# Scattering the experts' rows in waited groups, a later fourth expert, and the last additions on one engine

## The chip, the cores and the metric

The kernel runs on one core of a Trainium2 chip. The metric is the time of one execution on the device, in microseconds (us). The kernel before was run three times: 570.32 us is the median, 569.85 and 570.35 are the ends. One further execution was recorded by the hardware profiler, and all rows below are of that one.

## The reference

A decoder layer in float32 over 16 sequences of 64 tokens (1024 rows of 256): self-attention with 16 heads whose weights come as 4-bit codes with scales, cross-attention with 16 heads over a 64-wide context, and a mixture of experts. Each adds its result to x. The change touches the last part alone:

```python
scores = softmax(xt @ Wg.T)                       # 1024 x 16 experts
# best 2 of 4 groups of experts, then the best 4 experts of those
topi = top_k(masked, 4)[1]
weights = take_along_axis(scores, topi, axis=1)
combine = zeros((T, E)).at[arange(T)[:, None], topi].add(weights)
h = silu(einsum('td,eid->eti', xt, W1)) * einsum('td,eid->eti', xt, W3)   # 176 wide
expert_out = einsum('eti,edi->etd', h, W2)
y = einsum('etd,te->td', expert_out, combine)
z = silu(xt @ Ws1.T) * (xt @ Ws3.T) @ Ws2.T       # shared expert, 352 wide
return y + z
```

## The kernel before

Rows of tokens lie in eight tiles of 128 (`x[0]` to `x[7]`; tiles 0 to 3 are half 0, tiles 4 to 7 half 1). Every float32 operand of a matrix product is split into a high and a low part, and three products of parts stand for one; `parts_of` makes the two parts with a cast on ScalarE (ACT, L112) and a subtract on VectorE (DVE, L113). TensorE is PE, GpSimd is POOL, SyncE is SP.

**The mixture of experts** doesn't compute every expert for every token. Of sixteen experts, the last (`w_last`) is computed for all rows ("dense"), and its share is added by `add_last` (L950 to L954; its add is L952). Each other expert, 0 to 14, has 384 slots in a buffer `xd` in the chip's memory.

1. `send(half)` (L837) scatters the normalised rows of a half to the slots: for each of the four choices k, four indirect transfers of 128 rows each, issued by POOL (L842). The targets are in order of expert, so that choice k can only hold rows of experts from k up. The instructions that write `xd` are kept in `sent_rows`, and for each choice in `sent_for[k]`. `side_by_side` declares that these transfers need not wait for one another.
2. `expert_weights(e)` loads an expert's weights on SP's queue (L277) into one of two buffers with the tag "w123", and splits them into parts: a cast on ACT (L278), a subtract on DVE and one on POOL (L283; DVE for the first three experts).
3. `expert_inputs(e)` loads 384 rows back on SP's queue (L1255), after all transfers in `sent_for[k]` for k up to e have landed, and transposes them on PE: two times three transposes (L1265), each three followed by `parts_of` into `xs`. A small copy, `to` (L1270), keeps the rows' return addresses.
4. `expert_hidden(e)`: eighteen matmuls of 128x384 (the "ups", L104), silu on ACT (L1283, L1286), products on DVE (L1284, L1287), parts `hp`.
5. `send_outputs(e)`: for three blocks of 128 rows, five matmuls each, a copy `y` (L1299), and an indirect transfer on POOL (L1304), which scatters the block to `yd`: rows of a choice lie there by token.
6. `load_outputs(k)` loads the outputs of choice k from `yd`: four transfers of 256 KB on SP's queue (L1320) into buffers with the tag "got", of which there are nine, after every transfer to `yd` that was issued so far (`returned`) has landed. It is called after the sends of expert 11 + k.
7. `add_outputs(k)` adds weight times output to x, one instruction on DVE for a tile (L1334); for tiles 2 and 5 ACT scales (L1331) and POOL adds (L1332). At the end each tile of x is stored (L1392), the even ones by SP's queue and the odd ones by ACT's.

**The order of the work.** A planner puts the instructions of each engine in an order ahead of time, by estimated durations and by the dependences; `tc.issue_after(...)` gives it further bounds. The loop over e from 0 to 16 issues, at step e, the inputs and weights of expert e, the hidden part of expert e - 1 and the outputs of expert e - 2. For e of 1 and 2 the hidden part of the expert before is issued first, and the inputs wait in order for the end of its ups (`up_done`). For e above 2 the inputs are issued before the hidden part of the expert before, so that their transposes can lie among its ups. After the loop come the adds of the four choices and the dense expert's second half (tiles 4 to 7), whose hidden parts are `dense_hidden(w_last, 1, 0)` and `(…, 1, 1)`.

A branch for tokens that find no slot is in the program and is not taken with these inputs.

Of the kernel before, what the change touches and what calls it, by code (L numbers as in the profile page):

```python
# [25 lines left out]
F32 = mybir.dt.float32  # L26
# [3 lines left out]
AF = mybir.ActivationFunctionType  # L30
ALU = mybir.AluOpType
AX = mybir.AxisListType

B, S, D = 16, 64, 256
NT = B * S
NI = NT // 128
# [6 lines left out]
E, INTER, NGRP, TOPK, TOPKG = 16, 176, 4, 4, 2  # L43
# [4 lines left out]
W_COLS = W_UP + 2 * D  # L48
# [23 lines left out]
def decoder_layer(ctx: ExitStack, tc: tile.TileContext, a: dict, out: bass.AP):  # L72
    nc = tc.nc
# [17 lines left out]
    def av_tile():  # L91
        return ps_av.tile([128, 512], F32, tag="av", name="av")
# [24 lines left out]
    x = [t[:, i, :] for t in x_pairs for i in range(2)]  # L117
# [122 lines left out]

    yd = dram.tile([(E - 1) * SLOTS + TOPK * NT, D], F32, tag="yd", name="yd")

    def side_by_side(sent, others):

        for other in others:
            tc.declare_no_dep(sent, other, reason="each writes rows of its own")
        others.append(sent)

    def behind(read, writes):
        for w in writes:  # L250
            tc.add_manual_dep(
                read,
                w.name,
                mybir.DependencyInfo(mybir.DependencyClass.Sync, mybir.DependencyReason.DATA),
                reason="it reads rows of each",
            )
# [42 lines left out]
    def expert_output(ps, w, h_p, cols):  # L299


        w2 = [[p[:, W_UP + k * D : W_UP + (k + 1) * D] for p in w] for k in range(2)]
        h = [p[:, cols] for p in h_p]
        return matmuls(
            ps,
            [
                (h[0], w2[0][0]),
                (h[0], w2[0][1]),
                (h[1], w2[0][0]),
                (h[2], w2[1][0]),  # L310
                (h[2], w2[1][1]),
            ],
        )

    with ExitStack() as attn:
# [410 lines left out]
        rows = [None, None]  # L726
        sent_rows, sent_for = [], [[] for _ in range(TOPK)]
# [108 lines left out]

        def send(half, choices=range(TOPK), waits=()):  # L837

            to = targets[half]
            for k in choices:  # L840
                for i in range(4):
                    sent = nc.gpsimd.indirect_dma_start(  # L842
                        out=xd[: TOPK * NT + (E - 1 - k) * SLOTS],
                        out_offset=bass.IndirectOffsetOnAxis(ap=to[:, k, i : i + 1], axis=0),
                        in_=rows[half][i // 2][:, i % 2, :],
                        in_offset=None,
                    ).ins
                    side_by_side(sent, sent_rows)
                    sent_for[k].append(sent)
                    behind(sent, waits)  # L850

# [107 lines left out]
        with (  # L959
# [109 lines left out]
            def dense_weights():  # L1069

                parts = [
                    xw.tile([128, 2, 2, 4 * HQ], F32R, tag=f"w_q{n}", name=f"w_last{n}")
                    .rearrange("p a b c -> p (a b c)")[:, :W_COLS]
                    for n in range(2)
                ]
                up = xb.tile([128, 3, 2, 2, DC], F32, tag="w_s", name="w_last_up")
                down = xb.tile([128, 2, D], F32, tag="w_o0", name="w_last_down")
                for t, cols in (
                    (up.rearrange("p a b c d -> p (a b c d)"), slice(0, W_UP)),
                    (down.rearrange("p a b -> p (a b)"), slice(W_UP, W_COLS)),  # L1080
                ):
                    nc.sync.dma_start(out=t, in_=a["W123"][E - 1][:, cols])
                    parts_of(t, parts[0][:, cols], parts[1][:, cols])
                return parts
# [18 lines left out]
            def dense_gated(g, up, g2, up2):  # L1103
                h_p = [
                    xa.tile([128, 512], F32R, tag=f"roped1{n}", name=f"dense1{n}", bufs=1)
                    for n in range(2)
                ]
                h_p.append(xa.tile([128, 512], F32R, tag="q_r", name="dense2"))
                nc.vector.tensor_tensor(g, up, g, ALU.mult)
                parts_of(g, h_p[0], h_p[1])  # L1110
                nc.vector.tensor_tensor(g2[:64], up2[64:], g2[64:], ALU.mult)
                parts_of(g2[:64], h_p[2][:64], h_p[2][64:])
                return h_p
# [15 lines left out]
            for n in range(len(units) + 2):  # L1129
# [5 lines left out]
                qd, half = units[min(n, len(units) - 1)]  # L1135
# [52 lines left out]
                if n == 8:  # L1188
                    w_last = dense_weights()
                    with after(exps[-1]):  # L1190
                        routed.append(weights_of_choices(0))
                if n == 9:
# [30 lines left out]
                    with after(aimed, placed):  # L1223
# [4 lines left out]
                        h_p = dense_gated(*dense_ups)  # L1228
# [4 lines left out]
    fw = ctx.enter_context(tc.tile_pool(name="fw", bufs=2, reuse_waits="tile"))  # L1233
    fx = ctx.enter_context(tc.tile_pool(name="fx", bufs=2, reuse_waits="tile"))
    fh = ctx.enter_context(tc.tile_pool(name="fh", bufs=2, reuse_waits="tile"))
    fy = ctx.enter_context(tc.tile_pool(name="fy", bufs=2, reuse_waits="tile"))

    gated, up_done = [None], [None]

    def expert_weights(src, down_lo=nc.gpsimd):  # L1240
        return weight_parts(
            src,
            fw.tile([128, W_COLS], F32, tag="w123", name="w123"),
            [
                fw.tile([128, W_COLS], F32R, tag=f"w123{n}", name=f"w123{n}", bufs=3)
                for n in range(2)
            ],
            down_lo,
        )
# [63 lines left out]

    def load_outputs(k):

        tiles = []
        for n in range(NI // 2):
            t = fy.tile([128, 2, D], F32, tag="got", name="got", bufs=9)
            first = (E - 1) * SLOTS + (TOPK - 1 - k) * NT + n * 256
            got = nc.sync.dma_start(  # L1320
                out=t, in_=yd[first : first + 256].rearrange("(i p) d -> p i d", p=128)
            ).ins
            behind(got, returned)
            tiles.append(t)
        return tiles

    def add_outputs(k, got, cw):
        for i in range(NI):
            y, w = got[i // 2][:, i % 2], cw[i // 4][:, k, i % 4 : i % 4 + 1]
            if i % 3 == 2:  # L1330
                nc.scalar.activation(y, y, AF.Copy, scale=w)  # L1331
                nc.gpsimd.tensor_tensor(x[i], x[i], y, ALU.add)  # L1332
            else:
                nc.vector.scalar_tensor_tensor(x[i], y, w, x[i], ALU.mult, ALU.add)  # L1334

    def dense_hidden(w, half, n):
        return expert_hidden(w, [p[:, :, n * 256 : n * 256 + 256] for p in normed[half]], 256)

    def dense_output(w, h_p, half, n, add):
        for b in range(2):  # L1340
            ps = av_tile()[:, :D]
            expert_output(ps, w, h_p, slice(b * 128, b * 128 + 128))
            add(half, 2 * n + b, ps)
# [6 lines left out]
    ws, xs, hs, got = {}, {}, {}, {}  # L1350
    with tc.issue_after(lows[-1]), tc.issue_after(silus[-1]):
        ws[0] = expert_weights(a["W123"][0], nc.vector)
    for e in range(E + 1):
        if e in (1, 2):

            low = lows[-1]
            hs[e - 1] = expert_hidden(ws[e - 1], xs[e - 1][0], SLOTS)
        if e < E - 1:
            low = lows[-1]
            with tc.issue_after(up_done[0] if e in (1, 2) else low):  # L1360
                xs[e] = expert_inputs(e)
            if e >= 1:
                with tc.issue_after(low), tc.issue_after(silus[-1]):
                    ws[e] = expert_weights(a["W123"][e], nc.vector if e < 3 else nc.gpsimd)
        if e == 1:
            with tc.issue_after(gated[0]), tc.issue_after(silus[-1]):
                routed.append(weights_of_choices(1))
        if 0 <= e - 1 < E - 1 and e > 2:
            hs[e - 1] = expert_hidden(ws[e - 1], xs[e - 1][0], SLOTS)
        if e - 2 >= 0:  # L1370
            if e == E:

                with tc.issue_after(gated[0]):
                    h_p = dense_hidden(w_last, 1, 0)
            last = send_outputs(e - 2, ws.pop(e - 2), hs.pop(e - 2), xs.pop(e - 2)[1])
            if e - 2 == E - TOPK - 2:
                short = slots_are_short()
            k = e - 2 - (E - 1 - TOPK)
            if k >= 0:
                got[k] = load_outputs(k)  # L1380
    with ExitStack() as behind_last:
        for ins in (*last, gated[0]):
            behind_last.enter_context(tc.issue_after(ins))
        cw = [r[0] for r in routed]
        add_outputs(0, got[0], cw)
        dense_output(w_last, h_p, 1, 0, add_last)
        add_outputs(1, got[1], cw)
        dense_output(w_last, dense_hidden(w_last, 1, 1), 1, 1, add_last)
        for k in range(2, TOPK):
            add_outputs(k, got[k], cw)  # L1390
    for i in range(NI):
        (nc.sync if i % 2 == 0 else nc.scalar).dma_start(  # L1392
# [10 lines left out]
    with tc.If(short > 0):  # L1403
        w_over = [weights_without_slot(half, routed[half][2]) for half in range(2)]
        with tc.For_i(0, E - 1, 1) as e:
            w = expert_weights(a["W123"][bass.ds(e, 1)].rearrange("o p c -> p (o c)"))
            for half in range(2):
                dense_expert(w, half, add_over)

                t = fs.tile([128, 4, E], F32, tag="slot", name="w_next")  # L1410
# [105 lines left out]
```

## Time and profile before

| What | us |
|---|---|
| median of three runs | 570.32 |
| the profiled execution | 577.4 |
| its span, from the first instruction to the last | 575.5 |
| PE busy in the span | 540.3 (94%) |
| DVE busy | 400.2 (70%) |
| ACT busy | 279.3 (49%) |
| POOL busy | 230.6 (40%) |
| 16 sends of half 1 to `xd`, first start to last start | 439.40 to 460.24 |
| first output send of expert 0, last of expert 14 | 472.70, 556.00 |
| loads of the four choices, issued from | 544.41, 551.41, 554.70, 561.03 |
| the adds of the end on DVE | 552.59 to 571.16 |

Positions are microseconds from the start of the span. The mean granted clock of TensorE was 0.978 of the full one. A row of a timeline gives the start, the duration, the engine, the line of the kernel, the operation, the result and operands by the program's names, and in brackets how long the engine was idle before it and what ended that. A row of groups gives after the bar the busy time, the mean in ns of one instruction, and the idle time before them. A row of stretches gives for 10 us the busy time of each engine. In the rows of slices each digit is a fortieth of the span, in tenths busy.

### The profile page before, as it was taken

What the parts mean: (1) busy time and instruction counts of PE and PEld (TensorE: products, weight loads), DVE (VectorE), ACT (ScalarE), POOL (GpSimd) and SP (SyncE); (2) the same over time, 40 slices, a digit from 0 to 9 for tenths busy, and PEclk for the clock granted to TensorE, in tenths of its full rate; (3) what the DMA queues carried; (4) which work ended last, traced back from release to release, by engine and by line L of the source; (5) the groups of instructions that cost most, each with busy time, mean ns of one, the idle gap of its engine ahead of it and who ended that gap; (6) DMA issues with size and microseconds to landing.
All of it is one profiled execution on the core that took longest, in us unless ns stands there. A gap on an engine that the chain in (4) does not pass through costs nothing.

```text
span 575.5 us, 10603 instructions
## 1 busy us (share of the span) xinstructions
PE 540.3 (94%) x4013; PEld 446.7 (78%) x4013; DVE 400.2 (70%) x879; ACT 279.3 (49%) x524; POOL 230.6 (40%) x213
## 2 busy tenths in 40 slices
PE   7999999999999989999999999999999779999962
PEld 5889898888989876757778577685787669999951
DVE  6355566644655788848577586889777479999866
ACT  4677557575574431230432323152525187777551
POOL 4260500101001005426243444632544717888862
PEclk9999999999999999999999999999999789999995
DMA  8564431823200599482020000000511658777384
GB/s 227 145 166 146 111 109 39 227 86 112 75 1 1 167 250 308 111 239 52 2 70 1 8 1 1 0 31 0 188 50 68 202 169 285 240 245 238 122 279 152
DMA packets 56294, 70.83 MB, mean 123 GB/s; under 512 B 13872, under 2 KB 42768, under 8 KB 56240
## 3 DMA queue, kind: packets, MB, share of 16 engines
q1 hardware_dynamic: 51408, 58.71, 34.5%
q0 software_dynamic: 3696, 10.36, 4.7%
q10 hardware_dynamic: 1136, 1.05, 0.6%
q8 instruction: 33, 0.54, 0.4%
q14 instruction: 21, 0.17, 0.1%
HBM read 48.61 MB, written 21.86 MB: 122 GB/s over the span
## 4 chain that ended last, share of the span: by engine, by line
PE 81%; DVE 7%; issue 4%; DMA 3%; ACT 3%; POOL 1%; SPq 1%; DVEq 0%; ACTq 0%; POOLq 0%
PE mm L104 47%; PE mm L1005 7%; PE av L590 5%; PE av L104 5%; PE at L573 4%; PE at L343 3%; PE at L1028 2%; PE av L1041 2%; PE at L1265 2%; PE mm L439 2%; DMA bqkv<-in_bqkv 1%; PE mm L461 1%; DMA got<-yd 1%; DVE x L1334 1%; POOL roped L990 1%
## 5 line engine op out<-in xcount | busy, mean ns | idle before, releaser
L990 POOL TENSOR_TENSOR roped<-rt,rt 128x512 f32<-128x512 f32 x48 | 62.6, 1325 | 83.4 <-DVE rt L984 80.5
L984 DVE TENSOR_TENSOR rt<-mm,rope_q 128x512 f32<-128x512 f32 x96 | 61.4, 685 | 24.3 <-PE mm L104 23.6
L104 PE MATMUL mm<-xn,w_q 128*128 128x512 f32 x288 | 73.9, 403 | 0.5 <-ACT xn L222 0.5
L104 PEld LDWEIGHTS mm<-xn,w_q 128*128 128x128 f32 x288 | 52.2, 188 | 14.0 <-issue 1.8
L104 PE MATMUL mm<-xs,w 128*128 128x384 f32 x270 | 55.3, 354 | 7.0 <-ACT xs L112 5.8
L1304 POOL DMA_INDIRECT yd<-y,to x45 | 47.9, 1064 | 27.6 <-ACT y L1299 13.1
L104 PEld LDWEIGHTS mm<-xs,w 128*128 128x128 f32 x270 | 48.4, 198 | 9.0 <-ACT xs L112 6.6
L327 ACT ACTIVATE p<-p 128x512 f32<-128x512 f32 x32 | 20.1, 629 | 62.3 <-DVE p L326 62.3
L324 DVE TENSOR_REDUCE sm_m<-at 128x8 f32<-128x512 f32 x32 | 21.8, 680 | 37.1 <-PE at L573 36.2
L1005 PE MATMUL mm<-roped,w_s 128*64 128x512 f32 x192 | 46.4, 602 | 0.7 <-POOL roped L990 0.7
L522 POOL TENSOR_TENSOR wv<-code,scale 128x512 fp32r<-128x512 f32 x7 | 9.5, 1360 | 88.2 <-DMA scale<-in_scales 58.7
L613 DVE TENSOR_TENSOR x<-mm,x 128x256 f32<-128x256 f32 x64 | 26.0, 419 | 23.9 <-PE mm L104 21.9
L104 PE MATMUL mm<-wo,o 128*128 128x256 f32 x256 | 39.6, 295 | 0.0
L104 PE MATMUL av<-w,hp 128*128 128x256 f32 x225 | 35.2, 290 | 0.7 <-ACT y L1299 0.7
L104 PE MATMUL mm<-xn,wq 128*128 128x512 f32 x128 | 34.6, 405 | 0.7 <-ACT xn L222 0.5
L104 PE MATMUL mm<-wv,xn 128*128 128x256 f32 x256 | 35.2, 289 | 0.0
L104 PE MATMUL mm<-xn,wk 128*128 128x512 f32 x128 | 34.9, 404 | 0.0
L590 PE MATMUL av<-pt,v 128*128 128x128 f32 x256 | 34.5, 277 | 0.0
L104 PEld LDWEIGHTS mm<-wo,o 128*128 128x128 f32 x256 | 32.9, 190 | 1.5 <-issue 0.4
L590 PEld LDWEIGHTS av<-pt,v 128*128 128x128 f32 x256 | 32.0, 191 | 1.2
L104 PEld LDWEIGHTS mm<-wv,xn 128*128 128x128 f32 x256 | 31.8, 189 | 0.9
L104 PEld LDWEIGHTS av<-w,hp 128*128 128x128 f32 x225 | 30.6, 190 | 1.9 <-ACT y L1299 1.2
(216 smaller groups left out, 1145.8 us busy)
## 6 DMA issues: line engine op xcount, KB each, us to landing
w<-in_W SPq DMA_DIRECT2D x15, 640.0 KB
code<-in_codes SPq DMA_DIRECT2D x32, 256.0 KB
scale<-in_scales SPq DMA_DIRECT2D x32, 256.0 KB
xr<-xd SPq DMA_DIRECT2D x15, 408.0 KB
xd<-zeros SPq DMA_DIRECT2D x8, 720.0 KB
yd<-zeros SPq DMA_DIRECT2D x8, 512.0 KB
got<-yd SPq DMA_DIRECT2D x16, 256.0 KB
wq<-in_Wq SPq DMA_DIRECT2D x4, 512.0 KB
```

The lines of the kernel that those rows point to most:

```text
L104: m = nc.tensor.matmul(ps, lhsT=l, rhs=r, start=(n == 0), stop=(n == len(pairs) - 1))
L324: nc.vector.tensor_reduce(m, sc, AX.X, ALU.max)
L327: exps.append(nc.scalar.activation(p, p, AF.Exp, scale=scale).ins)
L343: last = nc.tensor.transpose(ps[:, 2 * n : 2 * n + 2, :].rearrange("p a q -> p (a q)"), pn[:, 2 * n : 2 * n + 2, :].rearrange("p a k -> p ...
L439: nc.tensor.matmul(ps[:, c * DCQ : (c + 1) * DCQ], lhsT=wq[:, h, c * 128 : (c + 1) * 128], rhs=wkq[:, h, :], start=True, stop=True,)
L573: nc.tensor.matmul(sc[par * 64 : par * 64 + 64, 2 * g + pp, :], lhsT=qk[0][:, b * S : (b + 1) * S], rhs=qk[1][:, b * S : (b + 1) * S], sta ...
L590: nc.tensor.matmul(av[:, k * 128 : (k + 1) * 128], lhsT=v[:, i, k0 : k0 + HD], rhs=pt[:, i].rearrange("p a q -> p (a q)"), start=True, sto ...
L613: nc.vector.tensor_tensor(x[i], ps, x[i], ALU.add)
L984: nc.vector.tensor_tensor(mt, ps3, rope_table(t, 2 * ab + k), ALU.mult)
L990: nc.gpsimd.tensor_tensor(r.rearrange("p (b s) -> p b s", s=S), one, two, op)
L1005: nc.tensor.matmul(ps[h // 2][(h % 2) * 64 : (h % 2) * 64 + 64], lhsT=w_s[:, t, blk, ab, :], rhs=roped[2 * t + ab], start=first[h], stop=l ...
L1304: sent = nc.gpsimd.indirect_dma_start(out=yd[: (E - 1) * SLOTS + min(TOPK, E - 1 - e) * NT], out_offset=bass.IndirectOffsetOnAxis(ap=to[:, ...
```

## The change

1. In `send`, the first transfer and the others of a group of four wait, for half 1 and choices 1 to 3, for the landing of the last transfer of the group before: `side_by_side` leaves that one out of the declaration.
2. For e of 3 too the hidden part of the expert before is issued first, and the inputs of expert 3 are issued after the end of expert 2's ups.
3. `add_outputs` does all tiles by the one instruction on DVE.
4. The outputs of the last choice (k of 3) are loaded into the two weight buffers "w123", two of 256 KB in each, and the second and fourth load are issued by ACT's queue.
5. The first two tiles of the dense expert's second half are issued before the adds of the first choice, and the other two before those of the second.

```diff
-    def side_by_side(sent, others):
+    def side_by_side(sent, others, landed=()):
         for other in others:
-            tc.declare_no_dep(sent, other, reason="each writes rows of its own")
+            if other not in landed:
+                tc.declare_no_dep(sent, other, reason="each writes rows of its own")
         others.append(sent)
...
             for k in choices:
+                landed = sent_rows[-1:] if half and k else ()
                 for i in range(4):
...
-                    side_by_side(sent, sent_rows)
+                    side_by_side(sent, sent_rows, landed)
...
     def load_outputs(k):
-        tiles = []
-        for n in range(NI // 2):
-            t = fy.tile([128, 2, D], F32, tag="got", name="got", bufs=9)
+        if k == TOPK - 1:
+            tiles = [
+                t[:, n * 2 * D : (n + 1) * 2 * D].rearrange("p (i d) -> p i d", i=2)
+                for t in (fw.tile([128, W_COLS], F32, tag="w123", name="got_last") for _ in range(2))
+                for n in range(2)
+            ]
+        else:
+            tiles = [
+                fy.tile([128, 2, D], F32, tag="got", name="got", bufs=9) for _ in range(NI // 2)
+            ]
+        for n, t in enumerate(tiles):
             first = (E - 1) * SLOTS + (TOPK - 1 - k) * NT + n * 256
-            got = nc.sync.dma_start(
+            got = (nc.scalar if k == TOPK - 1 and n % 2 else nc.sync).dma_start(
                 out=t, in_=yd[first : first + 256].rearrange("(i p) d -> p i d", p=128)
             ).ins
             behind(got, returned)
-            tiles.append(t)
         return tiles
...
-            if i % 3 == 2:
-                nc.scalar.activation(y, y, AF.Copy, scale=w)
-                nc.gpsimd.tensor_tensor(x[i], x[i], y, ALU.add)
-            else:
-                nc.vector.scalar_tensor_tensor(x[i], y, w, x[i], ALU.mult, ALU.add)
+            nc.vector.scalar_tensor_tensor(x[i], y, w, x[i], ALU.mult, ALU.add)
...
     for e in range(E + 1):
-        if e in (1, 2):
+        if e in (1, 2, 3):
             low = lows[-1]
             hs[e - 1] = expert_hidden(ws[e - 1], xs[e - 1][0], SLOTS)
         if e < E - 1:
             low = lows[-1]
-            with tc.issue_after(up_done[0] if e in (1, 2) else low):
+            with tc.issue_after(up_done[0] if e in (1, 2, 3) else low):
                 xs[e] = expert_inputs(e)
...
-        if 0 <= e - 1 < E - 1 and e > 2:
+        if 0 <= e - 1 < E - 1 and e > 3:
             hs[e - 1] = expert_hidden(ws[e - 1], xs[e - 1][0], SLOTS)
...
+        dense_output(w_last, h_p, 1, 0, add_last)
         add_outputs(0, got[0], cw)
-        dense_output(w_last, h_p, 1, 0, add_last)
-        add_outputs(1, got[1], cw)
         dense_output(w_last, dense_hidden(w_last, 1, 1), 1, 1, add_last)
-        for k in range(2, TOPK):
+        for k in range(1, TOPK):
             add_outputs(k, got[k], cw)
```

## The prediction

> **What bounds the kernel now.** I read, in order, the busy shares and the forty slices, the chain that ended last, the table of 10 us stretches from 430 us on (the only part that the change touches), and then the timelines of single engines around 460 to 480 us and from 552 us.
>
> ```profile
> PE 540.3 (94%) x4013; PEld 446.7 (78%) x4013; DVE 400.2 (70%) x879; ACT 279.3 (49%) x524; POOL 230.6 (40%) x213
> ...
> PE   7999999999999989999999999999999779999962
> DVE  6355566644655788848577586889777479999866
> PEclk9999999999999999999999999999999789999995
> ...
> PE 81%; DVE 7%; issue 4%; DMA 3%; ACT 3%; POOL 1%; SPq 1%; DVEq 0%; ACTq 0%; POOLq 0%
> ```
>
> TensorE sets the time, and is below nine tenths in two places after the start: slices 32 and 33 (about 446 to 475 us, where the experts' rows are sent and the first experts start) and the last two. The stretches say the same:
>
> ```profile
> 450.00:460.00 10.00, 7.87 (x34) 7.21 (x34) 5.48 (x13) 1.45 (x3) 7.95 (x7) 0.66 0.62 207
> 460.00:470.00 10.00, 6.68 (x34) 6.45 (x34) 6.98 (x21) 7.49 (x12) 0.96 (x1) 0.83 0.64 220
> 470.00:480.00 10.00, 8.62 (x57) 7.87 (x56) 9.70 (x21) 7.89 (x17) 6.09 (x6) 1.00 0.59 181
> 480.00:490.00 10.00, 10.00 (x74) 10.00 (x73) 9.18 (x17) 8.40 (x18) 6.63 (x7) 1.00 0.83 277
> 500.00:510.00 10.00, 10.00 (x70) 9.84 (x69) 9.69 (x16) 7.54 (x16) 8.74 (x7) 1.00 0.76 256
> 560.00:570.00 10.00, 3.21 (x10) 2.36 (x10) 9.84 (x19) 2.59 (x6) 4.05 (x5) 0.50 0.62 195
> ```
>
> (Busy us of PE, PEld, DVE, ACT, POOL, then granted clock, DMA share, GB/s.) From about 474 to 540 us PE and DVE are full, and POOL is close to it: time lost before it is not made up there, and time saved before it is kept. From 560 us it is DVE that is full.
>
> **A, sends by fours.** Three waits on POOL, no instruction more. Before, the sixteen sends of half 1 start 1.26 to 1.33 us apart, and then POOL has nothing to do:
>
> ```profile
> 460.24 0.96 POOL L842 DMA_INDIRECT xd<-rows,to  x1 [0.30 <-issue]
> 472.70 0.95 POOL L1304 DMA_INDIRECT yd<-y,to  x1 [11.50 <-ACT y L1299]
> ```
>
> By the semaphores' events the last send of each group landed 2.3, 3.4, 3.2 and 3.1 us after its start. So: the second choice's group starts at 445.9 (landing of the first's last) instead of 444.8, its last send starts at 449.7 and lands at 453.0; the third's lands at 460.1; the fourth's last starts at 463.9 and lands at 467.0, POOL is free at 464.9 instead of 461.2 (+3.7). Behind the waiting sends on POOL stands expert 0's first output send, wanted at 472.70: 7.8 us of cover. The loads of expert rows (L1255) on SP wait for the landings: expert 1's row load goes out at about 453.1 instead of 452.4 and lands at 457.3, needed by the transposes at 459.19; expert 2's at 460 to 461.5, needed at 469.02; expert 3's at 467 to 468, landing 471, needed at about 476. On SP the loads of weights stand behind these (w for expert 2 now ahead of expert 1's rows). Cost 0; without the cover up to 3.7. It could also gain: with one group in flight less, a landing may shorten, but nothing waits for it.
>
> **B, expert 3's rows later.** Moved behind expert 2's ups: one load of 408 KB on SP (now behind expert 3's weights), six transposes, two casts on ACT, two subtracts and the copy of `to` on DVE. Nothing is added. Before, three of the transposes ran inside expert 2's ups, and PE went on without a hole:
>
> ```profile
> 463.24 0.79 PE L104 MATMUL mm<-xs,w 128*128 128x384 f32 x3 [3.23 <-ACT xs L112]
> 471.41 0.80 PE L104 MATMUL mm<-xs,w 128*128 128x384 f32 x3 [1.10 <-ACT xs L112]
> 473.56 0.55 PE L1265 MATMUL at<-ident,xr 128*128 128x128 f32 x3
> 473.87 1.81 PE L104 MATMUL mm<-xs,w 128*128 128x384 f32 x9
> 475.64 0.49 PE L1265 MATMUL at<-ident,xr 128*128 128x128 f32 x3
> ```
>
> The first two lines are what this order costs: experts 1 and 2 have it already, with all six transposes after the ups of the one before, and their ups start 3.23 and 1.10 us late, behind an ACT cast. Expert 3 now gets it too. On ACT, before, its work came ahead of expert 2's silu:
>
> ```profile
> 473.25 1.26 ACT L278 CAST w<-w 128x1280 fp32r<-128x1280 f32 x1 [0.16 <-PE av L104]
> 474.42 0.47 ACT L112 CAST xs<-at 128x384 fp32r<-128x384 f32 x1
> ```
>
> After, ACT does the two silus first (0.50 + 0.48, the second ready at about 477.0, when the ups end), then the weights' cast (1.26, to 478.3), then the rows' (0.48 each, to 479.4), with the DVE subtract (0.51) behind. PE has meanwhile the transposes (0.82) and a part of expert 1's fifteen output matmuls (2.1 us if all are left, near nothing if they were already drawn ahead). So the hole is between 0.9 and 2.7 us; I take 1.8, between the two rows. Some 0.2 comes back, as the pieces of DVE and ACT work of the next step are done in it: 1.6 late. Who is late next: expert 3's ups, its outputs and sends, then each expert behind, by PE's order. To take it back, experts 4 to 14 would have to run faster than a pair per 11.7 us, and they have nothing to do so with: POOL has three sends at 1.26 plus a subtract of 1.31 to 2.06 for each, PE 9.6 to 10 of 10. Ends: 0 (the work hides wholly under expert 1's outputs) and 2.7. Which experts have their transposes inside the ups of which others shifts by one up to the end; I cost this at 0, with ±0.6 (half of the 1.10 row) for the last expert's start.
>
> **C, D, E, the end.** Removed: 8 ACT scales (505 ns) and 8 POOL adds. Added: 8 DVE adds. Moved: four loads of the last choice into weight buffers, two from SP's queue to ACT's; the dense outputs of the last expert (four L952 adds, ten matmuls) ahead of the first choice's adds in issue.
>
> ```profile
> L1334 DVE SCALAR_TENSOR_TENSOR x<-got,cw,x 128x256 f32<-128x256 f32 x24 | 12.5, 576 | 2.5 <-DMA got<-yd 2.4
> L1332 POOL TENSOR_TENSOR x<-x,got 128x256 f32<-128x256 f32 x8 | 6.1, 778 | 4.5 <-ACT got L1331 2.7 <-DVE x L952 0.9 <-DVE x L1334 0.8
> ...
> 563.39 1.83 DVE L1334 SCALAR_TENSOR_TENSOR x<-got,cw,x 128x256 f32<-128x256 f32 x2
> 565.25 0.97 DVE L113 TENSOR_TENSOR hp<-h,hp 64x256 fp32r<-64x256 f32 x1
> 569.50 1.66 DVE L1334 SCALAR_TENSOR_TENSOR x<-got,cw,x 128x256 f32<-128x256 f32 x4
> ```
>
> The last line is the undisturbed pace: starts 0.395 us apart. The two above it lie beside POOL adds and take twice as long; summed over the tail the stretched ones lose 3.0 us. The rule that speaks against C is in the Trainium skill, "Perfetto Trace Analysis", "Optimizing Scalar/DVE Operations": where DVE is saturated, giving work to ScalarE or even GpSimd can pay, though GpSimd and DVE share a port, so between these two it may not. DVE is saturated here (9.84 of 10). By the first half of the rule, taking eight adds back costs 8 x 0.395 = 3.2; by the rows, 3.2 - 3.0 = +0.2. I go by the rows.
>
> E only changes the order of issue; PE is idle for 4.23 us there, ahead of its matmuls at 560.86: 0. Where the adds end: the third choice's first load landed at 559.5, held by sends and transfers that don't change, and behind it DVE has 27 instructions after (21 before): 559.6 + 27 x 0.395 = 570.3. The last choice's loads wait for the last expert's sends to land (560.94), not for a buffer, so new buffers don't start them earlier; two queues may bring the last of them from 566.8 to about 565.5 (the third choice's end at 562.3, and 1 MB at the 0.8 us per 256 KB seen there). As their adds come early in DVE's order I allow a stall of 0.6. So the last add ends at 570.9, against 571.16: -0.3. On ACT, the cast of `hp` 64x256 (561.39 before) stands behind two loads that wait for 560.94: 0.6 late, with the last dense outputs behind it, before at 568.32: covered. Ends for the end: -2.0 (all stretching gone, no stall) and +1.5 (a stall of 2.4, as the 2.38 us wait for a load before 558.62 shows).
>
> **Sum.** A 0, B +1.6, end -0.3: +1.3 us on the profiled execution's 577.4 (575.5 between first and last instruction, 1.9 around them; the last add is 4.3 ahead of the span's end, and the output stores behind it stay). That execution is 7.1 us above the median of the runs, 570.32; as I carry only a difference of a part at the full clock, it goes over unscaled: 571.6.
>
> **The rivals.** Bound for "no change": 0.2%, 1.14 us, about what a measurement of this kernel can tell.
> - Late fourth expert kept to the end (above), 571.5 to 573: 0.40.
> - Nothing moves, 570.5: the hole is below 1 us, since DVE's and ACT's work for expert 3 fills it, and the end gives 0.3 back. For it: PE has 7 output matmuls to spare at 472.48. Against it: the rows of 3.23 and 1.10 had such matmuls as well. 0.28.
> - Other side, the end wins, 568.4: DVE with no POOL add beside it keeps 0.395 all through, and the two queues bring the last loads before DVE asks, -2.0, and the hole is near 0. It decides from the point where the end gains over 1.1 more than the hole costs. For it: six stretched lines. Against: 27 instructions behind 559.5. 0.22.
> - DVE becomes the bound of the end, 573.6: hole 2.0, and adds of the last choice placed ahead of others stall DVE, +1.3. 0.10.
>
> **How the numbers follow.** Faster is the third case: 0.22. Same is the second: 0.28. Slower: 0.40 + 0.10 = 0.50. Range 568.6 to 573.9: the cut faster case at the low end, the fourth case at the high, a tenth left out at each. The first case alone: 571.5 to 573.
>
> **What would show it.** A: half 1's sends in four groups with gaps of 1 to 3 us, expert 0's first output send at 472.7 still held by ACT's y. B: a wait of 0.9 to 2.7 us on ACT's xs ahead of expert 3's first three ups at about 477, and the last expert's sends later by as much. End: every DVE add at 0.42 to 0.48, no POOL after the last send, the last add 0.3 us earlier than the sends' lag would make it. Wrong if PE is as full at 470 to 480 as before, or if the last sends come no later, or if DVE waits for the last loads by over 1 us.

## The result, and the profile after

The changed kernel takes 572.85 us (median of five, 571.93 to 574.24) against 569.85 (569.52 to 570.35) before: 0.54% longer, 95% interval 0.42 to 0.66%. Measured again beside parts of the change it was 573.0 against 569.73: 0.66%, 0.45 to 0.88%. So it costs 3.0 to 3.3 us, where 1.3 were forecast; the sign and the range held.

Before takes about 570 us in most measurements, but the profiled execution of the first part took 577.4 and one set of runs below about 577 (the longest executions there, up to 589 us, are left out of the medians), so each kernel is compared with before as measured beside it, and traces with a second trace of before, of 569.12 us.

The page of the changed kernel (profiled execution 574.24 us):

```profile
span 572.5 us, 10586 instructions
...
PE 536.0 (94%) x4013; PEld 443.5 (77%) x4013; DVE 400.1 (70%) x887; ACT 276.1 (48%) x516; POOL 223.1 (39%) x205
...
PE   6999999999999989999999999999999769999961
...
DVE  5455556644565789758486686889778677999876
...
PE 70%; DVE 7%; POOL 7%; DMA 7%; issue 6%; ACT 2%; SPq 0%; DVEq 0%; POOLq 0%; ACTq 0%
PE mm L104 40%; PE mm L1009 7%; PE av L592 5%; POOL xd L846 5%; PE at L575 4%; PE at L345 2%; PE av L104 2%; PE at L1032 2%; PE mm L441 2%; PE av L1045 2%; DMA xd<-rows,to 2%; DMA yd<-y,to 1%; DMA bqkv<-in_bqkv 1%; POOL yd L1308 1%; PE mm L463 1%
```

The sends to `xd` are now on the chain that ended last: POOL at L846 with 5% of the span, and their landings with 2%. The stretches of 10 us (PE, PEld, DVE, ACT, POOL, granted clock, DMA share, GB/s) show PE's dent deeper at 460 us than in the second trace of before, here first:

```profile
450.00:460.00 10.00, 8.00 (x45) 7.05 (x45) 6.71 (x21) 6.10 (x10) 6.62 (x7) 1.00 0.68 223
460.00:470.00 10.00, 7.63 (x50) 6.83 (x50) 8.64 (x18) 8.13 (x16) 4.69 (x4) 1.00 0.90 290
470.00:480.00 10.00, 10.00 (x71) 9.97 (x70) 9.10 (x19) 7.93 (x17) 6.51 (x7) 1.00 0.88 281
```

and then the changed kernel:

```profile
450.00:460.00 10.00, 7.33 (x44) 6.80 (x45) 6.48 (x20) 6.23 (x10) 4.74 (x5) 1.00 0.37 136
460.00:470.00 10.00, 6.12 (x39) 5.17 (x37) 7.44 (x17) 6.59 (x13) 6.77 (x7) 1.00 0.69 230
470.00:480.00 10.00, 9.22 (x57) 9.22 (x58) 6.77 (x13) 6.58 (x15) 6.59 (x6) 0.83 0.93 330
```

PE is busy for 22.67 of these 30 us instead of 25.63. The timelines name it. POOL of the changed kernel, the first send of each waiting group, the last send and the first output send:

```profile
443.78 1.06 POOL L846 DMA_INDIRECT xd<-rows,to  x1 [1.73 <-DMA xd<-rows,to]
452.62 0.96 POOL L846 DMA_INDIRECT xd<-rows,to  x1 [3.48 <-DMA xd<-rows,to]
459.35 0.95 POOL L846 DMA_INDIRECT xd<-rows,to  x1 [1.73 <-DMA xd<-rows,to]
463.14 1.67 POOL L846 DMA_INDIRECT xd<-rows,to  x1 [0.30 <-issue]
465.12 0.96 POOL L1308 DMA_INDIRECT yd<-y,to  x1 [0.31 <-ACT y L1303]
```

and, in the second trace of before, the last send of half 1 and the same first output send:

```profile
457.48 0.96 POOL L842 DMA_INDIRECT xd<-rows,to  x1 [0.30 <-issue]
464.65 0.95 POOL L1304 DMA_INDIRECT yd<-y,to  x1 [6.20 <-ACT y L1299]
```

PE of the changed kernel, the transposes of experts 1, 2 and 3:

```profile
455.17 0.85 PE L1269 MATMUL at<-ident,xr 128*128 128x128 f32 x6 [2.43 <-DMA xr<-xd]
462.69 0.85 PE L1269 MATMUL at<-ident,xr 128*128 128x128 f32 x6 [2.32 <-DMA xr<-xd]
470.78 1.09 PE L1269 MATMUL at<-ident,xr 128*128 128x128 f32 x6 [2.07 <-DMA xr<-xd]
```

In the second trace of before:

```profile
454.31 0.85 PE L1265 MATMUL at<-ident,xr 128*128 128x128 f32 x6 [1.37 <-DMA xr<-xd]
461.88 0.84 PE L1265 MATMUL at<-ident,xr 128*128 128x128 f32 x6 [1.77 <-DMA xr<-xd]
465.69 0.55 PE L1265 MATMUL at<-ident,xr 128*128 128x128 f32 x3 [0.19 <-DVE xs L113]
466.00 1.81 PE L104 MATMUL mm<-xs,w 128*128 128x384 f32 x9
```

PE waits for the rows in both; expert 3's rows come just in time before, and 2.07 us late after, although their transposes now stand later in PE's order. To compare traces whose starts differ, I use three distances in us: from the first send of half 1 to the first output send of expert 0 (E0), from the same first send to the last output send of expert 13, and from that last output send to the end of the last add.

| Kernel | first send to E0 | first send to last send of expert 13 | from there to last add |
|---|---|---|---|
| before, first trace | 33.3 | 111.9 | 19.9 |
| before, second trace | 27.5 | 106.3 | 19.1 |
| eight adds alone, second run | 27.5 | 107.2 | 19.0 |
| end alone | 27.5 | 107.1 | 20.2 |
| expert 3 later alone | 27.5 | 108.8 | 19.0 |
| expert 3 later, and the end | 27.5 | 108.5 | 21.4 |
| waits alone | 28.5 | 114.0 | 18.8 |
| waits alone, queue as before | 27.6 | 112.6 | 20.2 |
| last wait alone | 27.5 | 110.3 | 19.1 |
| waits and expert 3 later | 28.2 | 110.5 | 19.0 |
| changed, first trace | 28.2 | 110.2 | 20.5 |
| changed, second trace | 29.1 | 109.9 | 19.9 |

Each row is one trace. Kernels that are alike in the middle column's part (before's second trace, adds, end) differ there by up to 0.9 us. In the last column the kernels with the end of before lie at 18.8 to 19.1, but two of them at 19.9 and 20.2, and the changed kernel's two traces are 0.6 apart. Differences that are no larger than these say nothing by themselves.

### The profile page after: what moved, and what is told of

The parts are those of the page before. It is cut to its first block, busy times and chain, and to the rows that moved or that the text cites. A ratio compares the mean times of both kernels' runs of the same rounds, so it can differ in the third digit from the quotient of the medians.

```text
span 572.5 us, 10586 instructions
## 1 busy us (share of the span) xinstructions
PE 536.0 (94%) x4013; PEld 443.5 (77%) x4013; DVE 400.1 (70%) x887; ACT 276.1 (48%) x516; POOL 223.1 (39%) x205
## 4 chain that ended last, share of the span: by engine, by line
PE 70%; DVE 7%; POOL 7%; DMA 7%; issue 6%; ACT 2%; SPq 0%; DVEq 0%; POOLq 0%; ACTq 0%
PE mm L104 40%; PE mm L1009 7%; PE av L592 5%; POOL xd L846 5%; PE at L575 4%; PE at L345 2%; PE av L104 2%; PE at L1032 2%; PE mm L441 2%; PE av L1045 2%; DMA xd<-rows,to 2%; DMA yd<-y,to 1%; DMA bqkv<-in_bqkv 1%; POOL yd L1308 1%; PE mm L463 1%
## 5 line engine op out<-in xcount | busy, mean ns | idle before, releaser
L104 PE MATMUL mm<-xs,w 128*128 128x384 f32 x270 | 53.9, 344 | 2.2 <-ACT w L280 1.3
L104 PEld LDWEIGHTS mm<-xs,w 128*128 128x128 f32 x270 | 46.0, 190 | 4.1 <-ACT w L280 2.2
L104 PEld LDWEIGHTS mm<-wv,xn 128*128 128x128 f32 x256 | 31.8, 189 | 0.9
```

The lines of the kernel that those rows point to most:

```text
L104: m = nc.tensor.matmul(ps, lhsT=l, rhs=r, start=(n == 0), stop=(n == len(pairs) - 1))
```

## The experiments

Line numbers of the changed kernel are 2 to 7 higher than those of before.

### Before once more

No edit.

> The kernel before once more, for a second trace. In the first one TensorE's granted clock fell to 0.66 in 450 to 460 us and to 0.83 in 460 to 470, and POOL's first send of half 1 stood 5.3 us behind the targets, where the changed kernel's trace has clock 1.00 and 3.5 us. Theory 'rows' (the sends by fours make TensorE wait for the rows of experts 1 to 3): without the drop in the clock the span is 2 to 4 us shorter than 575.5, and TensorE's waits on the row loads (DMA xr) ahead of the transposes of experts 1 to 3 sum to under 3 us, against the 7.2 of the changed kernel. Theory 'planner' (the later fourth expert costs the time): the waits on xr are 5 us or more here too.

569.12 us, span 567.3: 8.2 us shorter than in the first trace, where 2 to 4 were expected. The waits of TensorE on the row loads between 436 and 482 us (in us: sum, number, longest) are

```profile
PE at L1265 <- DMA xr<-xd: 3.7, 3, 1.8
```

and in the changed kernel's first trace

```profile
PE at L1269 <- DMA xr<-xd: 7.2, 4, 2.4
```

Of these 1.37 + 1.77 = 3.1 us belong to experts 1 to 3: a little over the 3 us expected, while the 'planner' theory wanted 5 or more. The changed kernel's second trace has 4.9 us in all, 1.2 more than before and not 3.5; there the clock fell to 0.75 in 455 to 460 us behind a wait of 2.97, and nine ups took 3.06 us, so that a part of the loss shows as slow matmuls instead of waits. The first trace of before had none of these waits. There PE stood still for another reason before the rows could be missed:

```profile
450.68 1.13 PE L104 MATMUL mm<-ws,sh 96*128 96x256 f32 x4 [1.65 <-issue]
```

and its clock was 0.66 in 450 to 460, so that expert 0 was 5.8 us later against the sends (first column of the table). That trace showed slack where the second has none.

### The waits alone

```diff
+    def side_by_side(sent, others, landed=()):
+        for other in (o for o in others if o not in landed):
...
+                    side_by_side(sent, sent_rows, sent_rows[-1 - i :][:1] if half and k else ())
```

> Only the waits of the sends in half 1, by fours; each engine's order stays, but on SP's queue expert 1's rows stand behind expert 2's weights and expert 3's weights ahead of expert 3's rows. Theory 'rows': slower by 1.5 to 2.5 us, TensorE waits about 2 us on xr at each of experts 1, 2 and 3. Theory 'planner', and the record's own step A: within 0.5 us of before.

576.16 us against 569.79: 1.16% slower (1.01 to 1.32), 6.4 us, over twice what I expected. The place is expert 3's three transposes, which in this order stand in front of fifteen of expert 2's eighteen ups:

```profile
470.93 0.87 PE L1265 MATMUL at<-ident,xr 128*128 128x128 f32 x3 [4.33 <-DMA xr<-xd]
471.45 3.23 PE L104 MATMUL mm<-xs,w 128*128 128x384 f32 x9
```

Behind the wait of 4.33 us the nine ups took 3.23 us; in the second trace of before the same nine took 1.81. The granted clock of the stretch (the value behind POOL's) says why:

```profile
470.00:475.00 5.00, 4.07 (x15) 4.10 (x16) 1.55 (x3) 0.48 (x1) 1.45 (x1) 0.50 1.06 396
```

So the waiting was paid once as idle time and once more as a halved clock. The Trainium skill, "TensorE: Matmul & The Clock Gate", "What's actually happening", has it that an idle window of about 3.4 us sets the array to half speed; this wait was longer, and the clock was at half. In the first trace of the changed kernel the clock fell too (0.83 in 470 to 480) where no single wait was over 2.4 us, so the length of one wait isn't all of it. The run with the last wait alone, below, shows it more plainly: nine ups took 3.23 us behind a wait of only 2.06.

### Expert 3's rows later alone

```diff
-        if e in (1, 2):
+        if e in (1, 2, 3):
...
-            with tc.issue_after(up_done[0] if e in (1, 2) else low):
+            with tc.issue_after(up_done[0] if e in (1, 2, 3) else low):
...
-        if 0 <= e - 1 < E - 1 and e > 2:
+        if 0 <= e - 1 < E - 1 and e > 3:
```

> Only expert 3's rows behind expert 2's ups, and the order that follows from it. The record's step B: +1.6 us, a hole of 0.9 to 2.7 us ahead of expert 3's ups. Theory 'rows': within 0.5 us of before, since TensorE then waits for rows at about this place anyway, or not at all.

571.11 against 569.79: 0.27% slower (0.14 to 0.41), 1.3 us by the medians. The prediction's step B holds: the hole at expert 3's ups was there,

```profile
471.53 0.79 PE L104 MATMUL mm<-xs,w 128*128 128x384 f32 x3 [0.83 <-ACT xs L112]
```

of 0.83 us (0.9 to 2.7 expected), and the last send of expert 13 comes 1.5 to 2.4 us later against the first send, so it is not made up behind.

### The end alone

All of `load_outputs`, `add_outputs` and the order of the end as in the change; nothing else.

> Only the end: all adds on VectorE, the last choice's loads into the weights' buffers over two queues, the dense outputs ahead in order. The record's step: -0.3 us. Theory 'end' (eight more adds behind the third choice's landing aren't given back): +0.7 us, as the changed kernel's last add ends 20.5 us behind the last send of expert 13, and 19.9 before.

570.54 against 569.79: 0.23% slower (0.11 to 0.35), 0.75 us by the medians. Theory 'end' fits in size. DVE of this kernel towards the end:

```profile
548.76 0.48 DVE L1337 SCALAR_TENSOR_TENSOR x<-got,cw,x 128x256 f32<-128x256 f32 x1
549.27 0.42 DVE L1287 TENSOR_TENSOR h<-mm,g 64x256 f32<-64x256 f32 x1
549.73 0.88 DVE L952 SCALAR_TENSOR_TENSOR x<-av,cl,x 128x256 f32<-128x256 f32 x2
552.56 0.88 DVE L1337 SCALAR_TENSOR_TENSOR x<-got,cw,x 128x256 f32<-128x256 f32 x2 [1.96 <-DMA got<-yd]
```

At 552.56 it takes up the third choice's first tile, after 1.96 us of waiting. By the program's order six adds of the first two choices still stand behind it (tiles 4 and 5 of the first, tiles 4 to 7 of the second).

### The waits and expert 3's rows later

Both edits above, the end as before.

> The waits by fours and expert 3's rows later, the end as before. Alone they cost 6.4 and 1.3 us. Theory 'cover' (with expert 3's transposes behind expert 2's ups, TensorE runs these eighteen matmuls while expert 3's rows are on their way, so that the wait of 4.3 us which they had in front of the ups shrinks to about 2): +1.5 to +2.5 us. Theory 'sum' (two independent costs): +7 to +8 us, which the end would have had to give back by 4 to 5.

575.18 against 576.86: 0.36% faster (0.19 to 0.53), where both theories expected it slower. They were meant against 570, and before took 577 here, so the total tests neither of them; the distance does. The last send of expert 13 comes 110.5 us behind the first send: 3.5 us less than with the waits alone (114.0), and 1.7 more than with expert 3 later alone (108.8). That fits theory 'cover' and not 'sum': alone the two cost 7.7 and 2.4 in this distance, together 4.2. The wait for expert 3's rows is 2.44 us here, behind expert 2's ups, not 4.33 in front of fifteen of them.

### The waits, with SP's queue as before

```diff
+        ).ins; loads.append(load)
...
-                with tc.issue_after(low), tc.issue_after(silus[-1]):
+                with tc.issue_after(low), tc.issue_after(silus[-1]), tc.issue_after(loads[e * 2 - 3] if e in (2, 3) else low):
```

> The waits by fours, with SP's queue held in the order of before (expert 1's rows ahead of expert 2's weights), so that the order of every engine is that of before and only the three waits are added. Theory 'weights' (the 640 KB of expert 2's weights, loaded 5 us earlier, lie among the second choice's rows and make them land late, 3.75 us of wait): the third group's wait falls to 2 us or less, everything behind comes 1.5 to 2 earlier, +4 to +5 us. Theory 'waits' (the three landings themselves): +6 to +6.8 as with the queue changed.

576.72 against 576.86, no difference (0.08% faster, from 0.23% faster to 0.07% slower), where 4 us or more were expected; before took 577 here too, so this total tests nothing either. By the traces, the waits of the sends on landings in this kernel:

```profile
POOL xd L842 <- DMA xd<-rows,to: 4.0, 2, 2.2
```

and in the one with the waits alone:

```profile
POOL xd L842 <- DMA xd<-rows,to: 5.5, 2, 3.7
```

The long wait, for the second choice's rows, falls from 3.75 to 2.23 us when expert 2's 640 KB of weights are not loaded among them, nearly to what 'weights' said, and the distance to expert 13's last send falls from 114.0 to 112.6. So, by one trace each, the load in front of the landing costs about 1.5 us of the distance, and the rest, 5.3 to 6.2, is the waits themselves.

### The eight adds alone, twice

```diff
-            if i % 3 == 2:
-                nc.scalar.activation(y, y, AF.Copy, scale=w)
-                nc.gpsimd.tensor_tensor(x[i], x[i], y, ALU.add)
-            else:
-                nc.vector.scalar_tensor_tensor(x[i], y, w, x[i], ALU.mult, ALU.add)
+            nc.vector.scalar_tensor_tensor(x[i], y, w, x[i], ALU.mult, ALU.add)
```

> Only the eight adds moved to VectorE. Theory 'end' (VectorE is the bound behind the third choice's loads): the stretched instructions, 3.1 us in the second trace of before, go; eight times 0.395 come: 0 to +1 us. The record's step gave +0.2.

576.08 against 576.86: 0.08% faster, from 0.29% faster to 0.13% slower. Once more, where before took 569.73:

> Only the eight adds moved to VectorE, once more. All of the end together cost 0.8 to 1.3 us where before ran at 570. Theory 'adds': +0.5 to +1.2, VectorE works without a gap from the third choice's load to the end and no instruction is stretched. Theory 'loads' (what costs is the last choice's loads, by their place in ScalarE's and SP's order): within 0.4 of before.

568.99 against 569.73: 0.08% faster, from 0.20% faster to 0.04% slower. So the adds are not what the end costs. The group of this kernel's adds (busy us, mean ns of one, idle us before them):

```profile
L1330 DVE SCALAR_TENSOR_TENSOR x<-got,cw,x 128x256 f32<-128x256 f32 x32 | 13.4, 478 | 2.0 <-DMA got<-yd 2.0
```

against, in the second trace of before,

```profile
L1334 DVE SCALAR_TENSOR_TENSOR x<-got,cw,x 128x256 f32<-128x256 f32 x24 | 13.2, 605 | 2.1 <-DMA got<-yd 2.0
```

32 adds at 478 ns keep DVE busy hardly longer (13.4 us) than 24 at 605 ns (13.2): what DVE does more, it had lost before in adds that took longer beside POOL's.

### The last choice's loads alone

The edit of `load_outputs` alone.

> Only the last choice's loads in the weights' buffers and over two queues, the adds as before. ScalarE's scales of tiles 2 and 5 and the cast of hp stand behind its two loads, which wait for the last expert's sends. Theory 'blocked ScalarE': +0.5 to +1.5 us. Theory of the record: 0, since the loads' start is set by the sends and their end is early enough.

577.53 against 576.86: 0.16% slower, from 0.04% faster to 0.36% slower. That holds both theories and doesn't decide between them.

### The changed kernel without the waits, and with them

The changed kernel once more:

> The changed kernel beside the parts of it, on one chip. From the first send of half 1 to the last output send of expert 13 its first trace has 110.2 us, before (second trace) 106.3, the waits alone 114.0 to 114.9, expert 3's rows later alone 108.8. Theory 'cover': 110 to 110.6 again, and +2.5 to +3.5 us against before where before runs at about 570. Where before itself runs at about 577 (TensorE's stall of 1.65 us at 449 us and the fallen clock behind it, as in the first trace), the waits keep that stall away, and the changed kernel is level with before or up to 2 us faster.

573.0 against 569.73: 0.66% slower (0.45 to 0.88), 3.3 us; distance 109.9. Without the waits of the sends:

> The changed kernel without the waits of the sends. Theory 'cover' (with expert 3's rows later, the waits cost only what lies beyond the hole that the later rows make anyway): the waits' own share of the change is 1 to 2 us, so this is 1 to 2 us faster than the changed kernel where before runs at about 570, with 108.5 to 109.2 us from the first send to expert 13's last. Theory 'waits are free inside the change' (the record's step A, if expert 3's order covers them): within 0.5 of the changed kernel.

572.25: 0.48% slower than before (0.32 to 0.64), 2.5 us; distance 108.5. The waits' own share inside the change is thus 0.75 us by the medians, 1.4 by the distances: between the two theories, and far from the 6.4 that the waits cost alone. It isn't clear of noise: the two kernels were run six times each, from 571.94 to 575.52 us and from 571.61 to 573.21.

### The last wait alone

```diff
+                    side_by_side(sent, sent_rows, sent_rows[-1 - i :][:1] if half and k == 3 else ())
```

> Only the wait ahead of the fourth choice's four sends; expert 3's weights move ahead of expert 3's rows on SP's queue, every other engine's order is that of before. The fourth group starts about 2.5 us later. In the second trace of before, expert 3's rows were there just in time (the transposes waited 0.2 us, for VectorE). Theory 'just in time' (each us that expert 3's rows land later is one that TensorE stands in front of expert 2's ups): +1.5 to +3 us. Theory 'slack' (the record: rows at 471, needed at 476): within 0.5 of before.

572.68 against 569.73: 0.55% slower (0.39 to 0.71), 3.0 us, at the upper end of 'just in time'. The fourth group started after a wait of 3.85 us, and PE waited for expert 3's rows as with all the waits, only for less:

```profile
468.59 0.87 PE L1265 MATMUL at<-ident,xr 128*128 128x128 f32 x3 [2.06 <-DMA xr<-xd]
469.12 3.23 PE L104 MATMUL mm<-xs,w 128*128 128x384 f32 x9
```

Behind it the same nine ups took 3.23 us again; the clock was 0.65 in 465 to 470 and 0.67 in 470 to 475. There was no slack at expert 3's rows.

## Why the prediction was right, and where it was not

**The sum.** Forecast +1.3, measured +3.0 and +3.3. The number is in the range of the likeliest case (the late fourth expert kept to the end, 571.5 to 573), but in part by luck: the late expert came at 1.3 us, which by itself would have lain just under that range (571.1), and the rest came from two terms that the forecast put at nothing and at a gain.

**A, the waits: 0 forecast, 0.75 us measured inside the change, 6.4 alone.** The step that failed is "expert 1's row load ... lands at 457.3, needed by the transposes at 459.19; expert 2's at 460 to 461.5, needed at 469.02; expert 3's at 467 to 468, landing 471, needed at about 476". Counted from the first send, expert 3's rows were to be loaded at about 28 us, to land at 31.6 and to be needed at 36.6. In the changed kernel's first trace they were loaded at 30.4 and PE, ready for them at 31.8, got them at 33.9. So both ends were off, the need by more. The times at which rows are needed were read from a trace in which PE had lost 5.8 us just before: in the second trace PE takes expert 3's rows 28.6 us behind the first send (465.69 less 437.12), where the first had 34.2 (473.56 less 439.40). The landings are late because the prediction names expert 2's weights, now ahead of expert 1's rows on SP, and puts them at no cost: with them the third group of sends waited 3.48 us for the second's landing, with SP's queue as before 2.23, and the forecast had 2.3 (453.0 less 449.7 and 0.96).

The cover on POOL was too large as well. It was 7.8 us in the forecast, behind sends that were to end 3.7 us later. In the second trace of before POOL is idle for 6.20 us there, and the sends of the changed kernel end 6.6 us later (27.9 us behind the first send against 21.3). All of the cover is used up, and the first output send comes 0.7 to 1.5 us later against the first send.

**B, expert 3's rows later: +1.6 forecast, +1.3 measured alone.** Right in size and in place when alone, with a hole of 0.83 us, just under the 0.9 that was its least. In the changed kernel itself that hole isn't there: its place is taken by the wait for expert 3's rows in front of the transposes (2.07 us in the first trace, 0.82 in the second), and the ups behind them wait for nothing. What the forecast didn't see is that A and B are not a sum: B moves the waiting transposes behind fifteen matmuls, and so pays for most of A.

**The end: -0.3 forecast, +0.75 alone, +1.1 on top of B (572.25 against 571.11, not measured side by side, so roughly).** The step C, taking eight adds back for +0.2, held: no measurable change. The length of the last stretch held too: from VectorE's first add of the third choice to the last add, 11.3 us forecast (559.6 to 570.9), 11.4 in the end alone (552.56 to 563.94). What failed is "the third choice's first load landed at 559.5 ... 559.6 + 27 x 0.395": the stretch is 1.7 us longer than before (9.7 in the second trace, 552.89 to 562.59), and the forecast let it begin 1.6 us earlier than before's first such add (561.20 in the first trace), which would have paid for it. Measured, it began 0.65 earlier: 8.8 us behind the last send of expert 13 in the end alone, 9.45 in the second trace of before. 1.7 less 0.65 is the 1.0 that the last column of the table shows (20.2 against 19.1); it is one trace each, within that column's scatter, so that the end's cost rests on the medians and the traces only say where it may lie.

Since the adds alone cost nothing, the cost is in the last choice's loads and the changed order (D and E). DVE's waits for loads at the end go with it: 2.01 us in the second trace of before, 1.98 with the adds alone (0.73 and 1.25), 2.67 with all of the end (1.96, 0.51 and 0.20). That is 0.7 more. My reading of it, from these traces and not tested by a run, is the order: the dense outputs issued first put the first choice's adds of tiles 4 and 5 behind them in the order of x, and the planner then placed a third-choice add, which waits for a load, ahead of them. With the adds alone DVE had 14 adds done when it came to wait for the third choice, for 0.73 us; with all of the end 10, for 1.96 us. Against that, the last choice's loads are waited for less (0.71 against 1.25). How much D and E cost one without the other stays open: the run with the loads alone didn't decide it.

**The rivals.** "Nothing moves" and "the end wins" both needed the hole below 1 us; the hole at the ups was 0.83, yet expert 13 came 1.5 to 2.4 late. The clock, 0.83 in 460 to 470 us of that trace, isn't the main reason: with expert 3 later and the end the hole is 0.83 too, the clock was 1.00 from 450 to 480 us, and expert 13 is still 1.3 to 2.2 late. That leaves the six transposes, which now lie in one piece ahead of the hole, and the subtract; they were not measured apart. "DVE becomes the bound of the end", 573.6, was nearer in total than the chosen number; its stall (0.76 us of waiting for the last loads) was not of the size it named.

## What to carry to other kernels

Before a wait is costed at nothing, read the slack from a trace whose own time agrees with the median: one that lost time upstream shows room that the others don't have, and shows it for every wait at once. Then ask what stands behind the waiting instruction in its engine's order: three transposes in front of fifteen matmuls made the same late rows cost 6.4 us, and the same transposes behind them 0.75 to 1.4. And when all last additions go to one engine, look at the order in which it takes them: here an add that waits for a transfer stood ahead of six whose turn had come before. That moving it back would gain is my reading, and was not tried.

## What the runs showed of the hardware that was not expected

- The landing of a group's last send of 128 rows released the next group 1.7 to 2.2 us after that send had left POOL, and 3.4 to 3.9 us after it where a 640 KB load had been issued 0.5 to 1.2 us before the last of the four.
- The waiting of TensorE was paid twice: nine matmuls of 128x384 took 3.23 us behind a wait of 4.33, at a granted clock of 0.50, against 1.81; and 3.23 again behind a wait of 2.06.
- Ahead of expert 0's transposes PE stood still for 1.65 us in the first trace of before with nothing shown that it waited for, and for 1.66 and 2.37 us in the traces of the eight adds alone (first run) and of the last choice's loads alone. In the traces with the waits taken beside these it was 0.57 us (waits and expert 3 later) and nothing (queue as before). Whether the sends in one run cause that stop was not tried; it stays open, and the change may be worth something where the stop occurs.
